# A two-layer graph network on one core: longer lags in the edge stage, norms moved ahead in the tile periods, and a block of VectorE work spread over eight steps

## The chip, the cores and the metric

The kernel runs on one core of one Trainium2 chip. A time is the device time of one execution in microseconds (us). Five engines of the core matter here: TensorE (PE in the profile, with its weight loads as PEld), VectorE (DVE), ScalarE (ACT), GpSimd (POOL) and SyncE (SP, which only issues transfers). Each works through its own instructions in the order in which they stand in the program, and waits on semaphores for the others. PSUM is where TensorE writes its results; a PSUM tile can be written again only when VectorE or ScalarE has read it.

## The reference, cut to what matters

625 nodes with 1024 features (`x`), 10,000 edges (`src`, `dst`), everything in float32. Layer 0 adds a graph attention (edge scores over 4 heads), a linear attention (16 heads of 64) and then a ternary feed-forward block to `x`. Layer 1 adds a two-step neighbour mean (SAGE), a linear attention and a mixture of experts.

```
# layer 0, graph attention
msg = xl[src] + xr[dst]
e   = einsum('ehd,hd->eh', where(msg > 0, msg, 0.2 * msg), att)
p   = exp(e - m[dst]);  alpha = p / (segment_sum(p, dst)[dst] + 1e-16)
out = segment_sum(alpha[..., None] * xl[src], dst).reshape(n, 256) @ W_up
# linear attention, both layers: qf, kf = elu(.) + 1
z   = 1.0 / (einsum('bthd,bhd->bth', q, k.sum(axis=1)) + eps)
out = einsum('bthd,bhdm->bthm', q, kv) * z[..., None] @ W_o + b_o
# the layers
xn = layernorm(x);  x = x + gnn0(xn, edges) + mix0(xn)
x  = x + ffn0(layernorm(x))                  # quantised activations, ternary weights
xn = layernorm(x);  x = x + sage(xn, edges) + mix1(xn)
x  = x + moe(layernorm(x))
```

## The kernel before, in words

`attempt` (the function under the launch) computes all of it; the nodes are cut into five tiles of 125 rows. Until the second half of layer 1 the order of the instructions on every engine is written out by hand. The helper `do` (class `Stream`, line 173) carries it: each call first runs the next waiting step of the calls before it (`after`, `after2`: reading out a PSUM tile, as a rule), then issues its own TensorE work (`pe`). So VectorE's and ScalarE's work on a result stands one or two steps behind the matmuls that made it.

**Edge stage** (lines 550 to 670; about 50 to 410 us of the span). TensorE makes keys and values of the linear attention (`key`, `value`), counts edges with one-hot matmuls (`pct`), makes the attention states (`states`), and then goes through eight queries and answers (`query`, `answer`). Beside that the 10,000 edges are scored in 40 groups of two columns of 128 edges (the last is 16 edges). Each group needs four indirect gathers on GpSimd (`ga`, `gb`, line 573), five VectorE instructions (`score_group`, line 577, and `score`, 553), one exponential on ScalarE (line 560) and two indirect scatters into `table` in DRAM on GpSimd (`scatter`, 584). The function `work` (607) places them: every step of TensorE credits an estimate of its time, and with every 8.0 us of credit one beat is issued.

```
while beat["us"] >= 8.0 * beat["g"] and beat["g"] < len(groups) + 3:
    ...
    if 2 <= g < len(groups) + 2:
        score_group(g - 2)
    for j in range(G):
        if g < len(groups): gather(g, j)
        if g >= 3: scatter(g - 3, j)
```

So a group is gathered in beat g, scored in beat g+2 and scattered in beat g+3. The buffers `ga` and `gb` exist four times: the gathers of a group wait until the group four before it is scored. Scatters follow each other in `table`: each waits until the one before it has landed. `self_loops` (596) writes the diagonal of `table` in beats 1 to 5. `states` reads each of its four PSUM tiles with three VectorE instructions (lines 288 to 291). `answer` takes a reciprocal of 128x626 on VectorE.

**Tile periods** (lines 937 to 988; about 430 to 630 us). After the last scatter GpSimd loads `table` back tile by tile (`load_table`), VectorE multiplies it with the edge counts (`weigh`, five instructions on 125x500), TensorE sums with it (`sums`), turns the result (`turn_sums`) and multiplies it with `W_up` into the same PSUM tile that holds the linear attention's output product (`mixed`, then `up_again`). In period p the kernel runs the sums of tile p, the feed-forward block of tile p-1 (`ffn`: `p1` norm and quantisation on VectorE, `f1` transposes, `f2` to `f4` matmuls with their read-outs) and the second norm of tile p-2 (`p5` on VectorE, `f5` transposes into `xnT1`). `spacer` puts two pieces of other TensorE work into each period: halves of `mixed` of tile p+2, or from p = 3 on a `key` and a `value` of layer 1. Two PSUM tiles (`ps1`) of one bank and three (`ps2`) of two banks serve all of this.

**Layer 1's answers** (lines 1038 to 1055; about 735 to 850 us). Eight queries and answers again. Beside the first two answers VectorE and ScalarE make the ten blocks `xnh`, `xnl` (normalised rows as a high and a low part, `split`, line 1016), five blocks beside each; then TensorE sums over neighbours (`pa`). `degrees` (993) makes the reciprocals of the node degrees earlier.

From 850 us on (second half of layer 1, attention and experts) nothing is touched by the change.

Of the kernel before, what the change touches and what calls it, by code (L numbers as in the profile page):

```python
# [52 lines left out]
def attempt(ctx: ExitStack, tc: tile.TileContext, w: dict, out: bass.AP, shifted: bool):  # L53
# [161 lines left out]
    class LinearAttention:  # L215
# [59 lines left out]
        def states(self):  # L275


            kf, v, kv = self.kf, self.v, self.kv[-1]

            def state(a):  # L280
                def pe():
                    hold["pkv", a] = ps1("pkv")
                    group(hold["pkv", a][:, :129], [(kf[:, t, a * 128:(a + 1) * 128], v[:, t, a, :])
                                                    for t in range(NT)])

                def after():
                    pkv = hold.pop(("pkv", a))
                    nc.vector.tensor_tensor(kv[:, a, 0:128], pkv[:, 0:128], blockmask, op=ALU.mult)
                    ks = mix.tile([128, 1], FP, tag="ks", name="ks", bufs=2)
                    nc.vector.tensor_copy(ks, pkv[:, 128:129])  # L290
                    nc.vector.tensor_scalar(kv[:, a, 128:256], blockmask, ks, None, op0=ALU.mult)

                do(None, pe, after)
                self.work(3.0)

            return [lambda a=a: state(a) for a in range(4)]
# [38 lines left out]
    with ExitStack() as st0:  # L335
        main = st0.enter_context(tc.tile_pool(name="l0", bufs=1))
        goT = main.tile([128, 2, N], FP, name="goT")
# [7 lines left out]
        with ExitStack() as edges:  # L345
# [207 lines left out]
            def score(dst, m, n, p):  # L553
# [4 lines left out]
                if not shifted:  # L558
                    nc.vector.tensor_scalar(dst, dst, LIMIT, None, op0=ALU.min)
                    nc.scalar.activation(dst, dst, AF.Exp)  # L560
# [35 lines left out]
            def self_loops(t):  # L596
# [3 lines left out]
                score(own[:, t:t + 1, :], m, 1, P)  # L600
                nc.vector.tensor_copy(xl1[:, t, :, 0:64], xlr[:, t, 0:256].rearrange("p (h e) -> p h e", h=4))
# [5 lines left out]
            def work(us):  # L607
                beat["us"] += us
                while beat["us"] >= 8.0 * beat["g"] and beat["g"] < len(groups) + 3:
# [4 lines left out]
                    if 2 <= g < len(groups) + 2:  # L614
                        score_group(g - 2)
                    for j in range(G):
                        if g < len(groups):
                            gather(g, j)
                        if g >= 3:
                            scatter(g - 3, j)  # L620
# [28 lines left out]
            for f in states[1]:  # L649
                f()  # L650
            for m in range(KC):
                if m + 1 < KC:
                    lin.query(m + 1)
                lin.answer(m, oT)
# [11 lines left out]
            while beat["g"] < len(groups) + 3:  # L666
# [36 lines left out]


        def mixed(t):
            for c in range(2):
                def pe(c=c):
                    if c == 0:
                        hold["px", t] = ps2("px1")
                    for k in range(KC):  # L710
                        nc.tensor.matmul(hold["px", t][:P, c, :], lhsT=oT[:, k, nodes(t)], rhs=wo[c](k),  # L711
                                         start=(k == 0), stop=False)

                yield lambda pe=pe: do(None, pe)
# [57 lines left out]
        def turn_sums(t):  # L772
# [6 lines left out]
            def after():  # L779
                nc.scalar.activation(goT[:, :, nodes(t)], hold["pt"][:, 0:2, :P], AF.Copy)  # L780
# [3 lines left out]
        def up_again(t):  # L784
            px = hold.pop(("px", t))

            def pe():
                for c in range(2):
                    for k in range(2):
                        nc.tensor.matmul(px[:P, c, :], lhsT=goT[:, k, nodes(t)],  # L790
# [34 lines left out]
        def ffn(t):  # L825
# [5 lines left out]
            hT = room[:, 256:384].bitcast(BF).rearrange("p (k n) -> p k n", k=2)  # L831

# [64 lines left out]
            def p5():  # L897
                stats(t, mv1, rs1)
                nc.vector.tensor_scalar(xq, x[:, t, :], mv1[:, t, 0:1], rs1[:, t:t + 1],
                                        op0=ALU.subtract, op1=ALU.mult)  # L900

            def f5():
                do(None, lambda: transpose_in(xnT1, t, xq))
# [6 lines left out]
        for f in mixed(0):  # L910
            f()
# [25 lines left out]
        for p in range(NT + 2):  # L937
# [3 lines left out]
            if p >= 2:  # L941
                made_of[p - 2][5]()
            spacer(p, 0)
            if p >= 2:
                made_of[p - 2][6]()
            if 1 <= p <= NT:
                made_of[p - 1] = ffn(p - 1)
                made_of[p - 1][0]()
            if p + 1 < NT:
                weigh(p + 1)  # L950
            if p == 0:
# [3 lines left out]
                                       lambda us: None, nc.gpsimd)  # L955
            if p + 2 < NT:
# [5 lines left out]
            if p < NT:  # L962
                sums(p)
            if 1 <= p <= NT:
                made_of[p - 1][1]()
                do()
                made_of[p - 1][2]()
# [25 lines left out]
    def degrees():  # L993
# [8 lines left out]
        def after():  # L1002
            nc.vector.tensor_scalar(halves(dinv), hold["pdeg"][:, :, :HN], 1.0, None, op0=ALU.max)
            if not shifted:
# [3 lines left out]
            nc.vector.reciprocal(dinv, dinv)  # L1008
            own = mix.tile([P, NP], FP, tag="qe", name="own", bufs=1)[:, 0:N].rearrange("p (t n) -> p t n", t=NT)
            nc.vector.tensor_tensor(own, dinv[:P, 0:N].rearrange("p (t n) -> p t n", t=NT),  # L1010
                                    ident[:P, :P].unsqueeze(1).to_broadcast([P, NT, P]), op=ALU.mult)
            nc.vector.tensor_reduce(dinvT, own, AX.X, ALU.add)

        do(None, pe, after)

# [22 lines left out]
    xnh = []  # L1038
    for m in range(KC):
        if m + 1 < KC:  # L1040
            lin1.query(m + 1)
        lin1.answer(m, oT)
        if m < 2:

            parts = [midp.tile([P, NT, 512], NUM, tag="mid", name="xnh")]
            parts.append(sage.tile([P, NT, 512], NUM, name="xnl") if m else
                         midp.tile([P, NT, 512], NUM, tag="mid", name="xnl"))
            for t in range(NT):
                xh = mix.tile([P, 512], FP, tag=("kb", "ke")[t % 2], name="xh", bufs=1)
# [780 lines left out]
```

## Time and profile before

| | |
|---|---|
| time, median of 3 runs | 2252.4 us (2249.21 to 2257.08) |
| the profiled execution's own time | 2253.43 us |
| its span, first to last instruction | 2251.6 us |
| TensorE matmuls busy | 2128.0 us (95%) |
| VectorE busy | 757.5 us (34%) |
| ScalarE busy | 195.6 us (9%) |
| GpSimd busy | 347.7 us (15%) |
| mean granted TensorE clock | 0.975 |

The busy times are sums over one execution; the page's second part cuts the span into 40 slices of 56 us and gives each engine's busy share in tenths. A row of waits names the engine and tile that stood still, the work that ended the wait, the total in us, the number of times and the longest. In the order of time ("the timeline") a row has start, duration, engine, line, operation and tiles, and in brackets the idle time of the engine just before it with what ended it. A float32 matmul stands as two rows.

### The profile page before, as it was taken

What the parts mean: (1) busy time and instruction counts of PE and PEld (TensorE: products, weight loads), DVE (VectorE), ACT (ScalarE), POOL (GpSimd) and SP (SyncE); (2) the same over time, 40 slices, a digit from 0 to 9 for tenths busy, and PEclk for the clock granted to TensorE, in tenths of its full rate; (3) what the DMA queues carried; (4) which work ended last, traced back from release to release, by engine and by line L of the source; (5) the groups of instructions that cost most, each with busy time, mean ns of one, the idle gap of its engine ahead of it and who ended that gap; (6) DMA issues with size and microseconds to landing.
All of it is one profiled execution on the core that took longest, in us unless ns stands there. A gap on an engine that the chain in (4) does not pass through costs nothing. (4 is left out here: it accounts for less than half of the span.)

```text
span 2251.6 us, 17442 instructions
## 1 busy us (share of the span) xinstructions
PE 2128.0 (95%) x6934; PEld 1217.9 (54%) x6934; DVE 757.5 (34%) x1305; ACT 195.6 (9%) x334; POOL 347.7 (15%) x351
## 2 busy tenths in 40 slices
PE   8989888888799899999999999999999999999998
PEld 6555455444454568764445776556754444444443
DVE  5878668764522561001013233322111111111112
ACT  2000001012210210000000111110000000000000
POOL 1667767400000040010000000110000000000010
PEclk9989988989999899999999999999999999999999
DMA  9343252521122110231213111030288997898742
GB/s 297 104 144 100 64 189 85 135 69 38 38 85 66 46 57 1 75 116 61 75 38 103 38 38 38 19 102 10 84 315 322 331 331 282 323 331 301 263 148 94
DMA packets 145849, 301.63 MB, mean 134 GB/s; under 512 B 12370, under 2 KB 22436, under 8 KB 145754
## 3 DMA queue, kind: packets, MB, share of 16 engines
q1 hardware_dynamic: 123412, 243.18, 30.2%
q0 software_dynamic: 17664, 47.47, 7.1%
q10 hardware_dynamic: 4678, 9.72, 1.4%
q8 instruction: 58, 0.95, 0.2%
q14 instruction: 37, 0.30, 0.0%
HBM read 277.49 MB, written 22.84 MB: 133 GB/s over the span
## 5 line engine op out<-in xcount | busy, mean ns | idle before, releaser
L129 PE MATMUL pu<-w,xgT 128*128 128x512 f32 x768 | 333.9, 593 | 1.9 <-DVE xgT L1124 1.9
L129 PEld LDWEIGHTS pu<-w,xgT 128*128 128x128 f32 x768 | 144.1, 190 | 174.7 <-issue 171.9
L129 PE MATMUL pyb<-w,hb 128*128 128x512 f32 x384 | 174.3, 599 | 2.4 <-ACT yb L104 2.1
L129 PE MATMUL pq<-xnT,w 128*128 128x313 f32 x512 | 150.7, 457 | 16.4 <-ACT qf L311 11.4
L129 PE MATMUL pk<-w,xnT 128*125 128x512 f32 x320 | 142.6, 599 | 4.7 <-DVE x L893 4.7
L129 PE MATMUL pv<-w,xnT 128*125 128x512 f32 x320 | 140.7, 592 | 0.0
L129 PEld LDWEIGHTS pq<-xnT,w 128*128 128x128 f32 x512 | 104.6, 205 | 61.6 <-ACT qf L311 13.3
L129 PE MATMUL p<-tT,w 128*128 128x313 f32 x512 | 136.3, 428 | 0.4 <-DVE tT L1124 0.4
L1664 DVE TENSOR_TENSOR su<-pu,su 128x512 f32<-128x512 f32 x24 | 16.6, 691 | 314.6 <-ACT su L1663 314.6
L129 PEld LDWEIGHTS pyb<-w,hb 128*128 128x128 f32 x384 | 69.9, 189 | 90.9 <-issue 74.8
L129 PEld LDWEIGHTS p<-tT,w 128*128 128x128 f32 x512 | 96.8, 190 | 37.8 <-issue 1.2
L129 PEld LDWEIGHTS pk<-w,xnT 128*125 128x125 f32 x320 | 60.1, 190 | 79.6 <-issue 72.9
L129 PEld LDWEIGHTS pv<-w,xnT 128*125 128x125 f32 x320 | 59.4, 188 | 71.1 <-issue 70.5
L587 POOL DMA_INDIRECT table<-es,at x79 | 84.0, 1063 | 57.8 <-issue 24.2
L1647 POOL DMA_INDIRECT xg<-rows_d,slots x12 | 11.3, 943 | 524.8 <-PE pxg L1654 449.0
L573 POOL DMA_INDIRECT ga<-xl_d,si x79 | 80.7, 1021 | 31.7 <-issue 20.7
L573 POOL DMA_INDIRECT gb<-xr_d,di x79 | 80.6, 1021 | 24.1 <-issue 23.5
L711 PE MATMUL px<-w,oT 128*125 128x512 f32 x160 | 73.3, 614 | 5.5 <-DVE oT L330 3.8
L1020 DVE TENSOR_TENSOR z<-pz,z 125x512 fp32r<-125x512 f32 x10 | 6.9, 692 | 196.8 <-ACT z L1018 196.8
L129 PE MATMUL px<-w,hT 128*125 128x512 f32 x160 | 70.3, 592 | 0.0
L129 PE MATMUL px<-w,oT 128*125 128x512 f32 x160 | 70.3, 592 | 0.0
L129 PE MATMUL ph<-meanT,w 128*128 128x313 f32 x256 | 70.1, 426 | 0.0
(357 smaller groups left out, 2582.1 us busy)
## 6 DMA issues: line engine op xcount, KB each, us to landing
w<-in_eW_dram SPq DMA_DIRECT2D x144, 1024.0 KB
w<-in_L_Wk_dram SPq DMA_DIRECT2D x8, 1024.0 KB
w<-in_L_Wv_dram SPq DMA_DIRECT2D x8, 1024.0 KB
w<-in_L_Wq_dram SPq DMA_DIRECT2D x8, 1024.0 KB
w<-in_L_Wo_dram SPq DMA_DIRECT2D x8, 1024.0 KB
w<-in_W_self_dram SPq DMA_DIRECT2D x8, 1024.0 KB
w<-in_W_neigh_dram SPq DMA_DIRECT2D x8, 1024.0 KB
w<-in_sW_dram SPq DMA_DIRECT2D x8, 1024.0 KB
```

What stands on the lines that cost most here:

```text
L129: nc.tensor.matmul(dst, lhsT=lhsT, rhs=rhs, start=(i == 0), stop=(i == len(pairs) - 1))
L573: nc.gpsimd.indirect_dma_start(out=dst[0:p, j, :], out_offset=None, in_=src[:, :], in_offset=bass.IndirectOffsetOnAxis(ap=ix[0:p, lo + j:l ...
L587: nc.gpsimd.indirect_dma_start(out=table[:, :], out_offset=bass.IndirectOffsetOnAxis(ap=at[0:p, lo + j:lo + j + 1], axis=0), in_=es[0:p, l ...
L711: nc.tensor.matmul(hold["px", t][:P, c, :], lhsT=oT[:, k, nodes(t)], rhs=wo[c](k), start=(k == 0), stop=False)
L1020: nc.vector.tensor_tensor(low, src, high.bitcast(FP), op=ALU.subtract)
L1647: nc.gpsimd.indirect_dma_start(out=xg, out_offset=None, in_=rows_d[:, :], in_offset=bass.IndirectOffsetOnAxis(ap=slots[:, b:b + 1], axis=0))
L1664: nc.vector.tensor_tensor(su, pu[:, 0, :], su, op=ALU.mult)
```

## The change

Five edits to the schedule; no arithmetic is added or dropped.

1. Edge stage: a beat comes every 7.6 us of credit; a group is scored three beats after its gathers, its exponential is a step of its own one beat later, and its scatters come five beats after the gathers.
2. `states`: ScalarE copies each PSUM tile into `raw`; VectorE does the masking for all four at once, one step later.
3. Six of the eight parts of tile 0's `mixed` are issued before the last answer of layer 0.
4. Tile periods: `p5` and then `p1` stand at the head of a period, `weigh` and the additions of the bias `bo` come after `f2`; `p5` writes into buffers of its own (`xn1`) and `f5`'s two read-outs are both on ScalarE. `goT` becomes a tile of its own for each node tile.
5. Layer 1: the ten blocks of `xnh`, `xnl` are spread over six answers (2, 2, 2, 2, 1, 1); the degrees' reciprocals (`inverses`) move behind the block of answer 5; the last answer stands after the first of the neighbour sums.

```diff
 # states
                 def after():
-                    pkv = hold.pop(("pkv", a))
-                    nc.vector.tensor_tensor(kv[:, a, 0:128], pkv[:, 0:128], blockmask, op=ALU.mult)
-                    ks = mix.tile([128, 1], FP, tag="ks", name="ks", bufs=2)
-                    nc.vector.tensor_copy(ks, pkv[:, 128:129])
-                    nc.vector.tensor_scalar(kv[:, a, 128:256], blockmask, ks, None, op0=ALU.mult)
-                do(None, pe, after)
+                    nc.scalar.activation(raw[:, a, :], hold.pop(("pkv", a))[:, 0:129], AF.Copy)
+                def after2():
+                    mask = blockmask.unsqueeze(1).to_broadcast([128, 4, 128])
+                    nc.vector.tensor_tensor(kv[:, :, 0:128], raw[:, :, 0:128], mask, op=ALU.mult)
+                    nc.vector.tensor_tensor(kv[:, :, 128:256], raw[:, :, 128:129].to_broadcast([128, 4, 128]), mask,
+                                            op=ALU.mult)
+                do(None, pe, after, after2 if a == 3 else None)
 # work
-                while beat["us"] >= 8.0 * beat["g"] and beat["g"] < len(groups) + 3:
+                while beat["us"] >= 7.6 * beat["g"] and beat["g"] < len(groups) + 5:
...
-                    if 2 <= g < len(groups) + 2:
-                        score_group(g - 2)
+                    if 4 <= g < len(groups) + 4:
+                        lo, n, p = groups[g - 4]
+                        exp(es[0:p, lo:lo + n, :])
+                    if 3 <= g < len(groups) + 3:
+                        score_group(g - 3)
...
-                        if g >= 3:
-                            scatter(g - 3, j)
+                        if g >= 5:
+                            scatter(g - 5, j)
 # layer 0's answers
             for m in range(KC):
                 if m + 1 < KC:
                     lin.query(m + 1)
+                else:
+                    for f in mixed(0, range(6)):
+                        f()
                 lin.answer(m, oT)
 # ffn
             def p5():
                 stats(t, mv1, rs1)
-                nc.vector.tensor_scalar(xq, x[:, t, :], mv1[:, t, 0:1], rs1[:, t:t + 1],
-                                        op0=ALU.subtract, op1=ALU.mult)
+                for h in range(2):
+                    nc.vector.tensor_scalar(xn1[h], x[:, t, h * 512:(h + 1) * 512], mv1[:, t, 0:1], rs1[:, t:t + 1],
+                                            op0=ALU.subtract, op1=ALU.mult)
             def f5():
-                do(None, lambda: transpose_in(xnT1, t, xq))
+                def pe():
+                    for h in range(2):
+                        p = ps1("ptr").rearrange("p (c n) -> p c n", c=4)
+                        for c in range(4):
+                            nc.tensor.transpose(p[:, c, :P], xn1[h][:, c * 128:(c + 1) * 128], ident[:P, :P])
+                        nc.scalar.activation(xnT1[:, 4 * h:4 * h + 4, nodes(t)], p[:, :, :P], AF.Copy)
+                do(None, pe)
 # the tile periods
                 made_of[p - 2][5]()
+            if 1 <= p <= NT:
+                made_of[p - 1] = ffn(p - 1)
+                made_of[p - 1][0]()
             spacer(p, 0)
             if p >= 2:
                 made_of[p - 2][6]()
-            if 1 <= p <= NT:
-                made_of[p - 1] = ffn(p - 1)
-                made_of[p - 1][0]()
-            if p + 1 < NT:
-                weigh(p + 1)
...
+            if p < NT:
+                sums(p)
+            if 1 <= p <= NT:
+                made_of[p - 1][1]()
+                do()
+                made_of[p - 1][2]()
+            do()
+            if p + 1 < NT:
+                weigh(p + 1)
             if p + 2 < NT:
                 load_table(p + 2)
             for t in range(2 * p, min(2 * p + 2, NT)):
                 for c in range(2):
                     xc = x[:, t, c * 512:(c + 1) * 512]
                     nc.vector.tensor_tensor(xc, xc, bo[c][:P], op=ALU.add)
-            if p < NT:
-                sums(p)
-            if 1 <= p <= NT:
-                made_of[p - 1][1]()
-                do()
-                made_of[p - 1][2]()
 # layer 1's answers
+    def rows_of(c, t):
+        xh = mix.tile([P, 512], FP, tag=("kb", "ke")[t % 2], name="xh", bufs=1)
+        nc.vector.tensor_scalar(xh, x[:, t, c * 512:(c + 1) * 512], mv1[:, t, 0:1],
+                                rs1[:, t:t + 1], op0=ALU.subtract, op1=ALU.mult)
+        split(xh, xnh[c][0][:, t, :], xnh[c][1][:, t, :])
+
+    for m in range(KC - 1):
+        lin1.query(m + 1)
+        lin1.answer(m, oT)
+        for _ in range(2 if m < 4 else 1):
+            if rows_left:
+                rows_of(*rows_left.pop(0))
+        if m == 5:
+            inverses()
...
     for k in range(KC):
+        if k == 1:
+            lin1.answer(KC - 1, oT)
```

In the changed order of instructions GpSimd has eleven scatters in a row behind the last gathers (seven before) and four fewer among them; SyncE's transfers keep their order. VectorE's order in a period with a layer 1 `key` becomes `p5`, `p1`, then the `key`'s bias addition `kb`.

## The prediction

> **What bounds the kernel now.** I read the page first, then the stages, then who TensorE waits for, then the order of time around those waits.
>
> ```profile
> PE 2128.0 (95%) x6934; PEld 1217.9 (54%) x6934; DVE 757.5 (34%) x1305; ACT 195.6 (9%) x334; POOL 347.7 (15%) x351
> PEclk9989988989999899999999999999999999999999
> ```
>
> TensorE is the bound overall; all dips of its clock lie in the first 850 us. The windows by stage put a size on that (columns: PE, PEld, DVE, ACT, POOL busy, granted clock, DMA share, GB/s):
>
> ```profile
> 148.00:265.00 117.00, 98.75 (x342) 57.19 (x341) 88.65 (x186) 9.22 (x24) 85.77 (x83) 0.93 0.33 101
> 264.00:408.00 144.00, 119.53 (x392) 79.00 (x392) 104.92 (x128) 14.53 (x32) 97.02 (x95) 0.88 0.35 116
> 430.00:640.00 210.00, 172.87 (x620) 94.28 (x619) 105.02 (x208) 37.86 (x51) 4.62 (x9) 0.92 0.18 53
> 640.00:850.00 210.00, 194.73 (x656) 120.86 (x655) 93.77 (x113) 25.49 (x38) 27.46 (x17) 0.94 0.20 68
> 850.00:2251.00 1401.00, 1384.64 (x4244) 765.45 (x4242) 237.70 (x375) 86.26 (x138) 46.35 (x51) 1.00 0.43 154
> ```
>
> Added gap by gap from the timeline, TensorE idles 43.0 us in the edge stage, 37.1 in the tile periods and 15.3 around layer 1's answers. After most gaps of 2.2 us and more its clock runs at half for slices of 3.4 us; by the trace's clock record matmuls were busy for 42.0, 20.3 and 18.5 us in such slices, and half of that is lost: 21.0, 10.2 and 9.2 us. So 64, 47 and 24.5 us are there to be had, 136 in all. The waits say who ends the gaps:
>
> ```profile
> PE ptr L845 <- DVE go L767: 14.7, 4, 6.1
> PE pkv L129 <- DVE ks L290: 13.3, 4, 8.3
> PE pq L129 <- ACT qf L311: 11.4, 3, 5.0
> PE ptr L845 <- DVE room L823: 11.3, 4, 6.4
> PE po L129 <- DVE oT L330: 6.7, 3, 3.7
> ```
>
> All are read-outs late on a queue, but VectorE (34%) is not full: something else stands in its queue. In the edge stage it is a gather that has not landed (timeline, then the tile view of the gathers: total and times):
>
> ```profile
> 159.82 0.69 DVE L581 TENSOR_TENSOR ga<-ga,gb 128x512 f32<-128x512 f32 x1 [6.26 <-issue]
> 163.92 2.49 PE L129 MATMUL pkv<-v,kf 125*128 125x129 f32 x10 [8.35 <-DVE ks L290]
> ...
> DVE ga L581: 41.4, 12
> ```
>
> Behind that stands GpSimd. Its transfers' rows start 1.27 (gather after gather), 1.25 and 1.30 us apart (medians), and in the timeline group 8 starts at 119.42, group 36 at 361.66: 8.65 us a group. The waits over 0.3 us in this stretch add to 17.3 us; without them it is 8.03. GpSimd's queue is full 93% of the time. **The edge stage is bound by GpSimd's issue of transfers**, not by VectorE's order alone. Its tail:
>
> ```profile
> 392.99 0.97 POOL L587 DMA_INDIRECT table<-es,at  x1 [1.40 <-DMA table<-es,at]
> 395.86 0.96 POOL L587 DMA_INDIRECT table<-es,at  x1 [1.90 <-DMA table<-es,at]
> 409.24 0.89 POOL L163 DMA_DIRECT2D tb<-table  x1 [1.76 <-PE pm L129]
> ```
>
> Without gathers between them each scatter waits for the last one to land: seven in 18.97 us (390.27 to 409.24), 2.71 each. Only then is `table` loaded back.
>
> In the tile periods VectorE's own order is the obstacle (period 3):
>
> ```profile
> 524.33 0.69 DVE L247 TENSOR_TENSOR kb<-pk,bk_t 125x512 f32<-125x512 f32 x1 [3.76 <-PE pk L129]
> 532.24 4.83 DVE L730 TENSOR_TENSOR pT<-tb,CT 125x500 f32<-125x500 f32 x5
> 538.57 1.07 PE L845 MATMUL ptr<-ident,room 125*128 125x125 f32 x4 [5.03 <-DVE go L767]
> ```
>
> `weigh` (4.83 us) stands before `go`, which frees the PSUM tile that the second transpose needs.
>
> **The edge stage, worked out.** Lags and the `raw` copies let VectorE and ScalarE wait less; the number of transfers stays. So I follow GpSimd. Start: gathers at 55.6 as before. Until group 8 the ring of four buffers sets the pace: gathers of g need the scoring of g-4, now one beat back instead of two. VectorE passed old beats 6 and 7 at 97 and 111; new beat 7 (53.2 us of credit, 6.65 old beats) comes near 106, the scoring takes 3.6, so group 8 starts near 110 (9 earlier, mostly because no early scatter waits for `table<-own` or `es`). Then 31 groups of 8.03: 359. Of the 17.3 us of waits, those ended by `es`, `qf` or shown as "issue" should go (the exponential is one beat older, the scatter two); about 8 to 10 are scatters waiting for a scatter's landing while weights stream in, and stay: group 39 starts at 368 (before: 387.7), the tail at 370.5. The tail is now eleven scatters: 29.8 us. The first `tb` load issues near 400.5, only 9 us earlier. It lands after 9.0 us (median of its tile view), its second piece is issued 0.9 later: 411; `weigh(0)` 4.9: the sums start near 415.5. TensorE itself: the score of group 38, 3.65 us, runs before answer 7's reciprocal (0.84+4.07+0.81), so oT is complete near 378; weight sums end near 387 (score of group 39, 2.2, three reductions 6.7); then `mixed` of tiles 1 and half of 2, 20.8, and a half-clock slice 1.7: 409. So the load chain decides: 415.5 against 429.78. **Gain 14** (4 to 31, the two ends by the rivals A and B). `mixed` of tile 0 ahead of the last answer fills 10.3 us of TensorE under the reciprocal; it shortens the path only if GpSimd doesn't bound it, and counts nothing here. The states' twelve small instructions (0.28+0.15+0.29 each four) become two of 0.7 on VectorE and four copies on ScalarE: hidden as long as ScalarE isn't behind a late `es`.
>
> [...] In this stage GpSimd's transfers last 0.96 (median) and up to 1.45 us, the longer ones beside one-hot and scoring instructions of VectorE. [...] at the trace's worst, 1.45 instead of the mean 1.03, they would add 95. The change packs VectorE's work only 5% denser, so I keep the mean of the trace.
>
> **The tile periods.** Now `go` no longer waits for `weigh`, and `p1` follows `p5` without waiting for the transposes. Durations of the period-2 and 3 rows: statistics 1.28+0.21, root with hand-over 0.36, norm halves 0.54 each, norm 0.81, reduction 1.22, quantisation 0.75. Period 1: second transpose at 459.5 instead of 461.7, the end 3.3 earlier. Period 2: `xq` ready at 488.4, sums end at 491.1, `go` 0.8, second transpose at 492.1 instead of 498.8; no half-clock slice behind it; `weigh` ends at 503, `hT` at 504.7, still under `up_again`: 8.5. Period 3: here the `key` is the spacer, and its `kb` (frees the PSUM tile for the second transpose of `f5`) stands behind `p1`: 526.9 instead of 525.0, a new stall of 2.0; ScalarE then makes `ke` and `kb` (0.63 each) before the two `xnT1` copies that VectorE shared: 1.5 more before the sums. Second transpose at 534.4 instead of 538.6; `weigh` delays `v` and the next transpose by 1.0: 3.2 less a half-clock slice: 2.2. Period 4 had no `weigh`: -0.9. Period 5: 3.6. Period 6: -1.3. **Gain 15** (8 to 21). The fewer table loads of ScalarE (1.28 each) and the longer life of `xn1` and `goT` are hidden. `load_table` keeps its place behind `weigh` on GpSimd's queue; its buffers are then long free (before, 22.7 us of waiting cost nothing).
>
> *A rule on the stalls.* The trace halves the clock after a gap of 2.23 us (530), 2.43 (395) and 2.90 (459), not after 1.3 or 1.4. [...] by the trace each costs 1.7. I take the trace.
>
> **Layer 1's answers.** Five blocks in a row (1.95 us each, VectorE waiting for ScalarE in each) delayed z and oT: gaps 13.8, states 1.5, clock 9.2. Spread, an answer has on VectorE two blocks 3.9, qf 0.81, z to oT 5.8, against 10.55 us of TensorE: starting 1.65 us after the query's end that is some 0.4 late, four times: 1.6. Answer 5 gets `inverses` as well (reciprocal 4.07, product and reduction 1.6): oT is 4.1 late once, with a slice 1.7. The last answer no longer waits for its reciprocal: the first neighbour sum (5.3) covers it. GpSimd's additions of `b1` and `L1_bo` now start some 16 us later, under the neighbour sums; nobody reads `x` before 1000. Left: 7.5 of 24.5. **Gain 16** (10 to 21).
>
> **Sum.** 14 + 15 + 16 = 45 off the profiled execution's 2253.4 (span 2251.6): 2208.4. The median of the runs is 1.0 lower: **2207**.
>
> **The rivals.** (A) GpSimd keeps 8.65 us a group, waits and all: group 39 at 378, the first `tb` load at 410.5, the sums at 425.5; edge gain 4: 2217. For: part of the waits is the transfers' own; against: the longest ones were for `es` or `table<-own`. (B) GpSimd runs at its medians, 7.65: the load at 383.5, the sums at 398.5, edge gain 31: 2190. (C) In the periods the late `kb` and ScalarE's copies eat the gain: 0 there, 2222. (D) The ring: with one beat instead of two between a buffer's release and its next gather, GpSimd waits for VectorE in every group. Between groups 4 and 8 it ran at 9.2 us a group already. Each us more a group moves the table load, which has no cover left, by 31 us: from 9.5 on the whole gain of 45 is gone, at 10.0 it is 61 us over the forecast: 2268, slower. Against: once GpSimd is late, the buffer that it needs next was scored three groups ago. (E) No effect: every us taken from a wait comes back at the table load: 2252.
>
> **Chances.** Forecast 0.56 (2193 to 2216), A 0.14, B 0.14, C 0.10, D 0.04, E 0.02. One tenth is left out on either side: 2186 to 2230. 0.3% (7 us) is what this measurement can tell from no change. Faster by more 0.94, within 0.02, slower 0.04.
>
> **What would show it.** Group 39's gathers near 368 and the first `tb` load near 400 (A: 412, B: 385); TensorE idle before the first sums, with the clock at half behind it; no wait `ptr <- go` over 1 us, new ones `ptr <- kb` near 2 us in periods 3 to 5; one wait of about 4 us at `po` in answer 6. Wrong if GpSimd waits for `ga` buffers in most groups, or if the stages after 850 us change.

## The result, and the profile after

2240.8 us (2239.2 to 2245.4, five runs) against 2257.0 (2249.2 to 2257.6) for the kernel before: 0.9938 of its time, interval 0.9924 to 0.9952. The gain is 16 us, not 45, and the time lies above the forecast range of 2186 to 2230. The profiled executions lie closer together: their span went from 2251.6 to 2240.2, 11.4 us less. From the page after (engines' busy time; TensorE's clock in 40 slices) and the windows by stage:

```profile
PE 2124.3 (95%) x6934; PEld 1214.5 (54%) x6934; DVE 754.2 (34%) x1265; ACT 193.5 (9%) x349; POOL 346.7 (15%) x351
PEclk9998999898899999999999999999999999999999
```

```profile
148.00:265.00 117.00, 96.41 (x358) 56.33 (x356) 85.62 (x172) 9.46 (x27) 85.86 (x84) 0.93 0.32 100
264.00:422.00 158.00, 129.07 (x423) 81.69 (x424) 114.89 (x128) 15.64 (x36) 101.72 (x97) 0.89 0.32 104
430.00:640.00 210.00, 186.01 (x635) 103.54 (x634) 113.33 (x223) 33.79 (x52) 9.69 (x18) 0.92 0.26 75
640.00:850.00 210.00, 196.51 (x722) 125.44 (x721) 95.68 (x95) 26.24 (x44) 26.92 (x16) 0.98 0.17 60
850.00:2240.00 1390.00, 1373.30 (x4166) 753.86 (x4164) 234.19 (x367) 86.26 (x138) 46.42 (x51) 1.00 0.43 156
```

Only layer 1's window has a clearly better clock (0.94 to 0.98); the edge stage and the tile periods keep theirs. Cut at the same events in each trace (us; "first pk" is the first key product, "sums" are the products `pg`, a tile period ends with its `pdn`, and `ph` is the first product behind layer 1's answers):

| kernel | first pk to first sums | sums to end of period 1 | end of period 1 to last pdn | to layer 1's first query | that query to first ph | rest |
|---|---|---|---|---|---|---|
| before | 384.6 | 48.1 | 141.3 | 109.2 | 137.0 | 1386.3 |
| after | 383.1 | 51.2 | 130.7 | 109.6 | 131.9 | 1386.2 |

The gains are 1.5, -3.1, 10.6, -0.3, 5.1 and nothing behind; the first pk itself came 2.4 us later, with the first loads (it lies between 45.0 and 48.6 in all runs). The sum is the span's difference, 11.4.

**Edge stage.** GpSimd's queue at the end of the stage, then VectorE's and TensorE's first work with the table (timeline):

```profile
389.05 1.02 POOL L592 DMA_INDIRECT table<-es,at  x1 [0.30 <-issue]
...
410.47 1.81 POOL L592 DMA_INDIRECT table<-es,at  x1 [1.89 <-DMA table<-es,at]
...
410.94 1.23 DVE L725 TENSOR_SCALAR gu<-raw 128x2048 bf16<-128x2048 f32 x1
...
413.69 2.31 POOL L592 DMA_INDIRECT table<-es,at  x1 [1.41 <-DMA table<-es,at]
...
414.66 1.23 DVE L725 TENSOR_SCALAR gu<-raw 128x2048 bf16<-128x2048 f32 x1
...
417.91 1.78 POOL L592 DMA_INDIRECT table<-es,at  x1 [1.91 <-DMA table<-es,at]
...
418.38 1.23 DVE L725 TENSOR_SCALAR dn<-raw 128x2048 bf16<-128x2048 f32 x1
...
421.40 0.89 POOL L163 DMA_DIRECT2D tb<-table  x1 [1.70 <-DMA table<-es,at]
...
429.57 4.85 DVE L743 TENSOR_TENSOR pT<-tb,CT 125x500 f32<-125x500 f32 x5 [9.97 <-DMA tb<-table]
...
430.68 0.43 PE L129 MATMUL pg<-xl,pT 125*125 125x65 f32 x2
...
431.62 0.43 PE L129 MATMUL pg<-xl,pT 125*125 125x65 f32 x2 [0.51 <-DVE pT L743]
```

The gathers of group 39, the last, start at 386.7 (before 387.7, forecast 368), the table load at 421.4 (before 409.2, forecast 400). From the first of the eleven scatters in a row to the load it takes 32.4 us (forecast 29.8). The sums then start before `pT` is complete and pause four times for 0.5 us, once for each further block; TensorE's clock is at half from 435.9 to 442.7.

**Tile periods**, period 3 (timeline):

```profile
520.58 0.68 DVE L247 TENSOR_TENSOR kb<-pk,bk_t 125x512 f32<-125x512 f32 x1
...
521.32 0.65 PE L924 MATMUL ptr<-ident,xn 125*128 125x125 f32 x4 [1.93 <-DVE kb L247]
...
523.12 5.21 PE L129 MATMUL pg<-xl,pT 125*125 125x65 f32 x30 [1.16 <-ACT xnT L925]
```

`go` is no longer late (longest wait of `ptr` for it 0.6). The stall at `kb` has the forecast size, 1.93 or 1.94, in periods 3, 4 and 5. But the slow slices behind it, by the trace's clock record, last 10.2 and 13.7 us in periods 3 and 4 (524.6 to 534.9, 558.8 to 572.4); in period 5 it is 3.4.

**Layer 1's answers** (the ten blocks now stand beside six answers). First two steps of the loop; then a block and the reciprocals of answer 5, with what TensorE's answer 6 waits for (timeline):

```profile
754.65 0.81 DVE L333 TENSOR_TENSOR oT<-po,z 128x626 f32<-128x626 f32 x1
...
755.57 0.78 ACT L312 ACTIVATE qe<-pq,bq 128x626 f32<-128x626 f32 x1 [6.58 <-DVE oT L333]
...
766.49 0.81 DVE L333 TENSOR_TENSOR oT<-po,z 128x626 f32<-128x626 f32 x1
...
767.42 0.78 ACT L312 ACTIVATE qe<-pq,bq 128x626 f32<-128x626 f32 x1 [6.58 <-DVE oT L333]
...
805.70 2.35 POOL L1089 TENSOR_TENSOR x<-x,b_t 125x1024 f32<-125x1024 f32 x1 [9.23 <-DVE xh L1072]
...
806.32 2.28 DVE L1047 TENSOR_TENSOR xnl<-xh,xnh 125x512 fp32r<-125x512 f32 x1 [0.70 <-ACT xnh L1045]
...
812.61 2.63 DVE L1039 TENSOR_TENSOR own<-dinv,ident 125x625 f32<-125x625 f32 x1
...
817.05 1.40 PE L129 MATMUL pd<-qf,kv 128*128 128x313 f32 x4 [3.99 <-DVE z L331]
...
822.07 2.46 PE L129 MATMUL po<-qf,kv 128*128 128x313 f32 x4 [3.62 <-DVE oT L333]
```

ScalarE's `qe` of a later query waits for VectorE's `oT`: `qe` and `z` are one buffer (`mix`, tag "qe", one copy). So a query's `qe` can't be written before the answer two steps back is complete. The step is 11.85 us (767.42 less 755.57), longer than TensorE's 10.55.

### The profile page after: what moved, and what is told of

Same layout as the page of the kernel before. It is cut to its first block, busy times and chain, and to the rows that moved or that the text cites. A ratio compares the mean times of both kernels' runs of the same rounds, so it can differ in the third digit from the quotient of the medians.

```text
span 2240.2 us, 17398 instructions
## 1 busy us (share of the span) xinstructions
PE 2124.3 (95%) x6934; PEld 1214.5 (54%) x6934; DVE 754.2 (34%) x1265; ACT 193.5 (9%) x349; POOL 346.7 (15%) x351
## 5 line engine op out<-in xcount | busy, mean ns | idle before, releaser
L129 PE MATMUL pq<-xnT,w 128*128 128x313 f32 x512 | 143.2, 440 | 11.0 <-DVE v L268 9.7
L129 PEld LDWEIGHTS pq<-xnT,w 128*128 128x128 f32 x512 | 99.8, 196 | 54.1 <-DVE v L268 10.5
L1680 POOL DMA_INDIRECT xg<-rows_d,slots x12 | 11.4, 947 | 524.7 <-PE pxg L1687 449.0
```

The lines of the kernel that those rows point to most:

```text
L129: nc.tensor.matmul(dst, lhsT=lhsT, rhs=rhs, start=(i == 0), stop=(i == len(pairs) - 1))
L1680: nc.gpsimd.indirect_dma_start(out=xg, out_offset=None, in_=rows_d[:, :], in_offset=bass.IndirectOffsetOnAxis(ap=slots[:, b:b + 1], axis=0))
```

## The experiments

Theory: the scatters of the edge stage wait for each other, so the lags bring nothing there; the clock makes the stall at `kb` dear; layer 1's answers run in a loop over a shared buffer. The runs were made in four batches. In two of them (edge_old, no_gb, f5_ps2, l1_loop; tiles_l1, tail9, old_lags_mixed_late, l1_z), called disturbed below, the edge stage was some 40 to 50 us longer, in the kernel before too (2310 and 2305 us as a whole, against 2255 and 2257 in the other two). It isn't a chip's property: one chip ran an undisturbed batch (ctrl's) and a disturbed one (tiles_l1's). The disturbed runs are read by the stages behind the edge stage, and whole times only within their batch. The stages come from one profile of each kernel.

**The edge stage.** edge_old: old lags.

```diff
-  while beat["us"] >= 7.6 * beat["g"] and beat["g"] < len(groups) + 5:
+  while beat["us"] >= 8.0 * beat["g"] and beat["g"] < len(groups) + 3:
...
-      exp(es[0:p, lo:lo + n, :])          # group g - 4
...
-      score_group(g - 3)
+      score_group(g - 2)
+      exp(es[0:p, lo:lo + n, :])          # group g - 2
...
-      scatter(g - 5, j)
+      scatter(g - 3, j)
```

> The changed kernel, with the lags of the edge stage as before: a beat every 8.0 us, scored two beats after the gathers, exponential behind the scoring, scattered three beats after; all other edits stay. Theory 1 (GpSimd's queue sets the end of the stage, 8.7 us a group whatever the lags, and each scatter behind the last gather adds 2.7 to 2.9): four scatters fewer stand in the tail, so the first load of the table issues near 410 instead of 421.4, and the first sums (pg) come 5 to 12 us earlier than 430.7; whole time 2229 to 2236. Rival (the longer lags do help, by keeping VectorE and ScalarE from waiting): the pace of the groups falls back to 9 us and more, the first sums come near or behind 431, and the whole time is the changed kernel's 2240.8 or up to 10 above it.

Measured 2285.3 (0.9907 of before, 0.9884 to 0.9931); first pk to sums 428.3 us, with 434.0 and 434.3 in the two kernels of that batch that kept the new lags. The disturbance is larger than the effect. In an undisturbed batch the same lags (`best`, below) gave 390.3 against 383.9 for the changed kernel (ctrl): 6.4 later, where theory 1 said 5 to 12 earlier. Counted to the end of period 1, before any other edit of `best` acts, it is 435.1 in both, so the lags by themselves bring nothing. no_gb: no second gather; the kernel leaves the rows `xr[dst]` out.

```diff
-  for dst, src, ix in ((ab[g][0], xl_d, si), (ab[g][1], xr_d, di)):
+  for dst, src, ix in ((ab[g][0], xl_d, si),):
```

> The changed kernel without the second gather of each column: the rows xr[dst] are not fetched, and the score takes the row of xl twice (this part of the computation is changed). GpSimd issues 79 transfers fewer of 305. Theory 1 (GpSimd's issue bounds the edge stage): at 1.3 us each some 105 us less for GpSimd, so that TensorE and VectorE set the pace instead: the groups come at the beats of the program, the last gather near 330 instead of 386.7, the first sums 25 to 60 us earlier. Rival (VectorE's order, or the landing of the scatters one behind another, bounds it): gathers weigh little, the first sums move by less than 10 us.

Measured: 346.6 us from first pk to sums, 82 to 88 less than the others of its batch (disturbed), and still 37 less than the undisturbed 383.1 of the kernel after, inside the 25 to 60 of theory 1; last gather at 336.4; whole time 2199.0 (0.953, 0.9497 to 0.9564). GpSimd then waits 58 us between groups 8 and 39 and no longer sets the pace. With all gathers in it, GpSimd's queue does bound the stage.

two_tables: every second column goes to another table.

```diff
+  table2 = dram.tile([128 * 3080, 4], FP, name="table2")
...
-  out=table[:, :],
+  out=(table, table2)[j][:, :],
```

> The changed kernel, with every second column scattered into a second table in DRAM that nobody reads (the weights of those edges are left out of the result). A scatter then waits for the landing of the scatter two before it. Theory 1 (in the tail each scatter waits for the one before it to land, 2.8 us, and the first load of the table waits for all): the eleven scatters of the tail take 15 to 18 us instead of 31, the waits for a scatter's landing fall from 32 us to under 10, the pace of the groups comes to 8.1 to 8.5 us, and the first load of the table issues 15 to 30 us earlier relative to the first gathers. Rival (GpSimd itself needs 2.8 us for a scatter that no gather precedes): the tail stays at 30.

GpSimd's end in this kernel (timeline):

```profile
370.03 0.96 POOL L593 DMA_INDIRECT table<-es,at  x1 [0.61 <-issue]
371.30 1.15 POOL L593 DMA_INDIRECT table<-es,at  x1 [0.30 <-issue]
373.85 0.96 POOL L593 DMA_INDIRECT table<-es,at  x1 [1.40 <-DMA table<-es,at]
...
384.93 0.90 POOL L163 DMA_DIRECT2D tb<-table  x1 [1.71 <-DMA table<-es,at]
```

Its waits, first in the kernel after, then here (us in total, times, longest):

```profile
POOL table L592 <- DMA table<-es,at: 32.6, 18, 4.2
```

```profile
POOL table L593 <- DMA table<-es,at: 1.7, 2, 1.4
```

Group 8 to group 39 takes 251.3 us, 8.11 a group, against 8.78 after and 8.65 before; the eleven scatters, from the first to the load, 17.8 instead of 32.4 us (15 to 18 forecast); first pk to sums 363.4. The load comes 37 us earlier than after, more than the 15 to 30 of the forecast. Its whole time (2262.6, ratio 1.0034) isn't compared: the other data give the experts more work (832 products `pu` instead of 768), and the rest behind the first ph is 45 us longer. Between groups 8 and 39 what GpSimd's waits exceed 0.3 us by adds to 19.1 before, 20.3 after, and to nothing here (counting waits over 0.45), and before and after most lie at nearly the same places, 135 to 175, 291 to 303, 324 and 382 us. The trace's landing times say why: nine of the ten waits before, and ten of the twelve after, come behind a scatter that took 3.6 to 7.3 us to land, where the median is 2.2. In two_tables scatters land as late (up to 6.2 us), but nobody waits for them. With the scatters' chain cut the waits are gone: they were a scatter's waits for the landing of the scatter ahead. This is the cause.

**The tile periods.** f5_ps2 and f5_pair put both transposes of `f5` into one two-bank tile from period 3 on; f5_ps2 leaves each copy behind its own four transposes, f5_pair (shown, cut) issues all eight first.

```diff
+  both = ps2("ptr5") if t else None
+  halves_of = []
   for h in range(2):
-      p = ps1("ptr").rearrange("p (c n) -> p c n", c=4)
+      p = both[:, h, :] if t else ps1("ptr")
+      p = p.rearrange("p (c n) -> p c n", c=4)
...
-      nc.scalar.activation(xnT1[:, 4 * h:4 * h + 4, nodes(t)], p[:, :, :P], AF.Copy)
+      halves_of.append(p)
...
+  if t:
+      for h in range(2):
+          nc.scalar.activation(xnT1[:, 4 * h:4 * h + 4, nodes(t)], halves_of[h][:, :, :P], AF.Copy)
```

> The changed kernel, with both transposes of f5 in one two-bank PSUM tile (ps2) from period 3 on, so that the second need not wait for the release of the key's tile by kb. Theory 1 (the stalls at ptr <- kb, 1.93 + 1.16 us, and the half-clock slices behind them cost periods 3 to 5 some 3.4 and more each): these waits go, periods 3 to 5 are 8 to 12 us shorter together, the sum of the half-clock slices between 520 and 605 falls from 27 us to under 10; whole time 2229 to 2233. Rival (another read-out is late in the same place, the copies of xnT1 on ScalarE or go): the stall turns up at pg or at the next ptr, and the gain is under 4 us.

> The changed kernel, with both transposes of f5 in one two-bank PSUM tile from period 3 on, all eight transposes ahead of the two copies. Theory 1 (the second transpose waits for kb, and the pair of gaps of 1.93 and 1.16 us brings a half-clock slice of 10 us): no gap over 1.5 us between 520 and 605 us, no slice with over 4 us of matmuls in it, and each of periods 3 to 5 is 6 to 8 us shorter: 15 to 24 us less from the first sums to the last pdn. Rival (the clock drops anyway, or the copies on ScalarE and the sums' own wait take the place of the gap): under 6 us less.

Who TensorE waited for in the periods, f5_ps2:

```profile
PE ptr L926 <- ACT xnT L927: 11.2, 3, 3.7
```

The half-written tile ties the second transpose to ScalarE's copy of the first, which stands behind `ke` and `kb`: one gap of 3.7 us instead of 1.93 and 1.16, and the same loss (130.8 us from period 1 to the last pdn; whole time 2289.7, 0.9925 of before, 0.9899 to 0.9951). So its rival came true. f5_pair took the wait away. The window 520 to 540 in ctrl (the changed kernel in that batch) and in f5_pair, busy PE, PEld, DVE, ACT, POOL, then the clock:

```profile
520.00:540.00 20.00, 16.71 (x71) 12.67 (x71) 8.09 (x22) 2.69 (x5) 0.00 (x0) 0.74 0.00 1
```

```profile
520.00:540.00 20.00, 18.95 (x93) 11.90 (x92) 14.47 (x28) 5.36 (x8) 0.00 (x0) 1.00 0.01 1
```

More work fits into the same 20 us at full clock. Periods 3 and 4 last 29.5 us instead of 37.4; period 5 gains only 1.0, with a new wait of 1.99 us at `pgu` in it (none over 1.5 was forecast). The end of period 1 to the last pdn takes 113.8 instead of 130.5; from the first sums on it is 14.7 less, just short of the 15 to 24 of the forecast, because period 1, where the sums pause, took 2.0 more. Whole time 2224.7 (0.9861, 0.9846 to 0.9877) against 2244.0 of ctrl (0.9952, 0.9940 to 0.9965).

> The changed kernel, unchanged, so that the other kernels are compared with it on one chip. All theories: the stages from the first sums on last as in its first profile (tile periods 182 us less the half-clock slice at their start, first query of layer 1 to the first ph 132 us); the edge stage shows how far its 383 us are this chip's.

ctrl repeats the stages of the kernel after within 0.8 us.

**Layer 1's answers.** l1_loop: `z` in a buffer of its own and `inverses` back at the end of the read-out in `degrees`; l1_z: the buffer alone.

```diff
-  z = mix.tile([128, NP], FP, tag="qe", name="z", bufs=1)
+  z = (self.room or mix).tile([128, NP], FP, tag="z" if self.room else "qe", name="z", bufs=1)
...
+  inverses()                # in degrees
...
+  lin1.room = sage
...
-  if m == 5:
-      inverses()
```

> The changed kernel, with z in a buffer of its own in layer 1 (it shared one with qe), and with the degrees' reciprocals back in front of layer 1's answers. Theory 1 (a loop qe, qf, two blocks, z, reciprocal, oT, qe of 11.9 us an answer, closed by the shared buffer, is longer than TensorE's 10.55 us): queries and answers run at TensorE's pace, the waits po <- oT of 1.3 us in answers 0 to 3 and the 7 us at answer 6 go, and the stretch from the first query to the first ph takes 121 to 125 us instead of 131.9; whole time 2230 to 2234. Rival (VectorE's work in the answer is itself too long, buffer or not): the waits keep over 1 us in answers 0 to 3, and only the wait at answer 6 shrinks: 4 to 6 us.

> The changed kernel, with only z of layer 1 in a buffer of its own; the degrees' reciprocals stay at answer 5. Theory 1 (two separate causes: the loop over the shared buffer costs 1.3 us in each of answers 0 to 3 and at answer 6, and the reciprocals cost some 6 of the 7.6 us at answers 5 and 6 and the slow clock behind): the stretch from layer 1's first query to the first ph is 124 to 128 us, between 131.9 and the 121 of both edits. Rival (the loop is all, the reciprocals fit once the loop is broken): 121 to 122. Second rival (the reciprocals are all): 130 to 132.

What ScalarE's `qe` waited for between the first query and the first ph, after, then l1_loop:

```profile
ACT qe L312 <- DVE oT L333: 50.3, 6, 15.8
ACT qe L312 <- PE pq L129: 21.4, 2, 13.3
```

```profile
ACT qe L313 <- PE pq L129: 57.8, 8, 13.3
```

All eight now wait for their own product. The stretch is 119.3 us in l1_loop (131.9 after) and 123.2 in l1_z, just under its 124 to 128: the buffer is worth 8.7, the reciprocals some 4 more (with both edits the stretch lies between 117.8 and 121.1 in the eight kernels below). How much of the 4 is GpSimd's additions, beside which a subtraction and `own` took 2.28 and 2.63 us in the kernel after instead of 0.69 and 0.81, isn't separated. l1_loop: 2276.8 against 2310.5 of before (0.9890, 0.9859 to 0.9922).

**Together.** `best`: old lags with f5_pair and l1_loop. tiles_l1 (and tiles_l1_b in an undisturbed batch): the new lags with these two. old_lags_mixed_late and lags_mixed_late: all of tile 0's `mixed` behind the last answer again. edge_before: also the old `states`. tail9 (tail9_b): scatters four beats behind, and the weight sums' three reductions one each behind answers 4 to 6.

> The changed kernel with four edits: the lags and the beat of the edge stage as before, f5 in one two-bank PSUM tile with its transposes ahead of its copies, z of layer 1 in a buffer of its own, the degrees' reciprocals back in front of the answers. If all three causes hold (scatters in the tail, the wait for kb with its slow clock, the loop over the shared buffer), the sum is 5 + 18 + 12 = 35 us under the changed kernel of the same chip. If only the loop holds, 12; if the longer lags do help, 5 to 10 less than that sum.

> The changed kernel with its own lags, and with the three edits behind the edge stage alone: f5 in one two-bank PSUM tile with its transposes ahead of its copies, z of layer 1 in a buffer of its own, the degrees' reciprocals in front of the answers. Theory 1 (the three causes add up and the lags are worth what the first sums showed, 431.3 against 438.6 us with the old lags): 22 us less from the first sums to the last pdn, 11 less from layer 1's first query to the first ph, so 2205 to 2213, 2 to 9 under the kernel with the old lags. Rival (what is taken from the tile periods comes back in the edge stage or at their start, as a half-clock slice): 2214 to 2222.

> The same kernel as tiles_l1, with the scatters four beats behind the gathers instead of five, and the three reductions of the weight sums one each behind answers 4 to 6 of layer 0, where VectorE waits for gathers. Theory 1 (after the last gather two things end the edge stage together: the row of scatters before the table load, and VectorE's weight sums before TensorE's last 48 products): two scatters fewer are 5.6 us, the weight sums 4 us; the first table load issues near 416, pm 4 us earlier, and the first sums come 3 to 6 us earlier than in tiles_l1. Rival (the pace of the groups suffers from scatters that wait for an exponential, or VectorE's reductions delay scores and so gathers): the last gather comes 3 or more later, and nothing is gained.

> The kernel of `best` (old lags), with all of tile 0's mixed behind the last answer of layer 0, as it stood before the change. Theory 1 (mixed ahead of the last answer delays that answer by 12 us on TensorE; on VectorE the scores of the last groups and the weight sums then stand behind its reciprocal): pm comes 6 to 8 us earlier, near 408, and the first sums 4 to 7 us earlier than 438.6; 2208 to 2211. Rival (VectorE waits there for the last gathers anyway, so the order does not matter): pm moves by under 2 us, whole time 2213 to 2216.

> The kernel of tiles_l1 again, as the base of this batch: all edits of the change, with f5 in one two-bank PSUM tile, z in its own buffer and the degrees' reciprocals in front. If the edge stage is as in the first profiles (383 to 385 us from the first pk to the first sums): 2208 to 2216. If it is longer by some 50 us in all kernels of this batch, before too, the differences below stand only where they are over 10 us.

> As tiles_l1_b, with the whole edge stage as before the change: old lags, beat and states, all of mixed behind the last answer. Theory 1 (the edits of the edge stage together are worth next to nothing, since GpSimd's scatters wait for each other in both): within 3 us of tiles_l1_b. Rival a (the lags are worth 6 to 7 us, as the first sums of the kernel with old lags showed): 5 to 8 us slower. Rival b (they cost, by the longer row of scatters): 3 to 6 us faster.

> As tiles_l1_b, with all of tile 0's mixed behind the last answer of layer 0. Theory 1 (with the new lags the row of scatters and the table load end the stage, not TensorE): within 2 us. Rival a (mixed ahead of the answer fills TensorE's wait for the reciprocal): 4 to 8 us slower. Rival b (it delays the last answer and with it VectorE's weight sums, as where the lags are the old ones): 3 to 6 us faster.

> As tiles_l1_b, with the scatters four beats behind the gathers instead of five, and the three reductions of the weight sums one each behind answers 4 to 6 of layer 0. Theory 1 (the row of scatters before the table load, and VectorE's weight sums before TensorE's last products, end the stage together): first table load 5 to 6 us earlier, first sums 3 to 6 us earlier, 2204 to 2212. Rival (scatters then wait for exponentials, and the pace falls): last gather 3 us or more later, nothing gained.

| kernel | median us | ratio to before | first pk to sums | sums to end of period 1 |
|---|---|---|---|---|
| best | 2214.6 | 0.9812 (0.9797 to 0.9827) | 390.3 | 44.8 |
| tiles_l1_b | 2212.8 | 0.9802 (0.9783 to 0.9821) | 384.2 | 52.9 |
| edge_before | 2207.9 | 0.9788 (0.9773 to 0.9803) | 386.3 | 44.8 |
| lags_mixed_late | 2211.3 | 0.9807 (0.9791 to 0.9823) | 382.4 | 53.2 |
| tail9_b | 2208.2 | 0.9786 (0.9772 to 0.9800) | 380.2 | 52.6 |
| tiles_l1 | 2248.7 | 0.9746 (0.9712 to 0.9781) | 437.0 | 44.9 |
| tail9 | 2254.9 | 0.9777 (0.9744 to 0.9811) | 441.1 | 44.9 |
| old_lags_mixed_late | 2245.9 | 0.9753 (0.9719 to 0.9787) | 427.9 | 44.8 |

Three of the eight rows, the last, are from the disturbed batch. `best` is 29.4 under ctrl; 35 was the sum if all three causes held. From the end of period 1 on all eight agree within 2 us to the last pdn (113.6 to 115.0) and within 4 in layer 1's answers (117.8 to 121.1). All edits of the edge stage together, tiles_l1_b against edge_before, bring 2.1 us up to the sums and lose 8.1 in the period after. The kernel after, with the same edge stage, shows there the four pauses of 0.5 us at `pT` and the clock at half from 435.9 to 442.7. The medians differ by 4.9 in favour of the old stage, with overlapping intervals: rival b's size, but not certain. `mixed` alone is within 2 us, as theory 1 said. With the old lags it does delay the last answer (`best`, timeline):

```profile
408.92 6.67 DVE L707 TENSOR_REDUCE part<-raw 128x1 f32<-128x2048 f32 x3
...
415.65 0.59 PE L129 MATMUL pm<-part,ones 128*128 128x3 f32 x2 [5.97 <-DVE part L707]
```

In edge_before `pm` comes 4.8 us earlier after the first pk (362.5 against 367.3), but there `states` differs too. old_lags_mixed_late fell into a disturbed batch, so this effect alone wasn't settled. tail9_b shows the row of scatters: the load issues 370.5 us after the first pk instead of 374.3 (3.8 earlier, 5 to 6 forecast), the sums start 4.0 earlier (3 to 6 forecast), with the pace unchanged. In the disturbed batch tail9 was the slower of the two, with a pause of 19.9 us before one query, longer than any in the others of that batch.

edge_before (2207.9) and tail9_b (2208.2) beat both kernels: 49 us under before, 33 under the change.

## Why the prediction was wrong, step by step

Three terms of the sum were too large. The edge stage gained 1.5 us instead of 14 (and started 2.4 late), the tile periods 7.5 instead of 15, layer 1's answers 5.1 instead of 16.

- **Bound by GpSimd: right** (no_gb). **31 groups at 8.03 us and half of the waits: wrong**; group 39 comes 19 us behind its forecast. Group 8 is 4.4 of it (114.4 for 110). The pace without waits was nearly right (8.11 in two_tables, 2.5 us in 31 groups). Most of it, 11 us, is the waits: 20.3 instead of the 9 or so that I kept. I let the half go that the trace put down to `es`, `qf` or "issue". All but one of these (a gather's, 1.2 us) came behind a scatter that landed late, with a later event's name on them, and the lags don't touch that. This is rival A, 8.78 measured for its 8.65, and its load time was still 9 to 11 us early. Rival D didn't show: between groups 8 and 39 no gather waited over 0.3 us.
- **Eleven scatters for 29.8 us: 2.6 short.** The first eight took the forecast 2.7 each. The last three ran beside VectorE's `ternary` instructions (128x2048) and took 1.81, 2.31 and 1.78 us, where the median scatter takes 1.00; each ended 0.1 us behind the end of such an instruction (412.28, 416.00 and 419.69 behind 412.17, 415.89 and 419.61). That is longer than the 1.45 us that I had as the trace's worst. For the gathers, beside scoring and one-hot instructions, keeping the mean of the trace was right: it stayed (1.02 before and after).
- **The load chain decides: right**, but the sums' start was the wrong mark. They start on the first block of `pT` and pay the wait in period 1, with a half-clock slice behind it: forecast 3.3 gained there, 3.1 lost. Where the sums don't have to pause, period 1 takes 44.8 us instead of before's 48.1 (no_gb, two_tables, `best`): there the order of the instructions does bring its 3.3.
- **`go` and the order of the norms: right.** Period by period, 1 to 5, the gain was -3.1, 9.3, 1.5, -4.2 and 4.0 us; 3.3, 8.5, 2.2, -0.9 and 3.6 were forecast. With f5_pair's edit the order is worth 27.5 us from the end of period 1 to the last pdn.
- **The stall at `kb`: right in size** (1.93 and 1.16 for 2.0 and 1.5), **its clock priced too low:** 5.0 and 6.4 us lost in the slices of periods 3 and 4 (half of 10.06 and 12.74 us of matmuls) instead of 1.7 each; in period 5 the 1.7 held (half of 3.12). The trace before already had a shorter pause with a slow slice behind it than the 2.2 us that I took as the least: 1.92 us at 761.2, with the clock at half from 763.3, ahead of the next pause at 765.4.
- **Layer 1, 16 us: wrong**, 5.1 measured. I priced an answer by VectorE's queue (0.4 late) and missed that `qe` waits for `z`'s buffer; the loop makes it 1.3. Behind the reciprocals there are three waits (3.99 and 3.62 in answer 6, 2.26 in answer 7), not one of 4.1: I had put GpSimd's additions under the neighbour sums, but they ran beside the blocks and the reciprocals, and there the subtraction and the `own` product took 2.28 and 2.63 us instead of 0.69 and 0.81. l1_z and l1_loop show the two parts, 8.7 and some 4 us. The clock's gain, 9.2 to 3.3, came as hoped.

## What to carry to other kernels

Before pricing a schedule, list the buffers that its stages share: here the one copy that `qe` and `z` share made a loop of two engines' queues, and its 11.85 us, not TensorE's 10.55, were the pace. When a wait is put down to a short instruction of another engine, see whether the waits stay at the same places under another cause, and look at the landing of the transfer ahead; here that was the older, slower event behind them. Price a stall with the clock that follows it (5.0 us were lost behind the 1.93 and 1.16 of period 3), and mark a stage's end where its last wait is paid, not where its first instruction starts.

## What the runs showed of the hardware

- Half-clock slices came with pauses of under 2 us that stood close together. In the kernel after the clock was at half for 10.2 us from 524.6, behind pauses of 1.93 and 1.16 us (from 519.4 and 522.0); for 13.7 us from 558.8, behind one of 1.94 (from 556.8) and with one of 0.73 inside the slice (from 559.8); and for 6.8 us from 435.9, behind the four of 0.5 in the sums (431.1 to 434.5). f5_ps2's single pause of 3.7 us cost the same as the pair (10.2). In period 5, where no sums follow, the pair brought 3.4 us (after) or 6.8 (ctrl) and the single pause 3.4. So the pauses alone didn't give the length of the slice; what does is open.
- In the kernel after four VectorE instructions with two float32 operands in SBUF that started beside one of GpSimd's additions ran longer and ended 0.55 to 0.67 us behind its end: the subtractions at 794.73 and 806.32 (2.29 and 2.28 us; 0.69 without it; the second ended at 808.60, the addition at 808.05), `own` at 812.61 (2.63; 0.81 in the kernel before; 815.24 and 814.58) and `qf` at 823.62 (1.40; 0.81 without it). `oT` and `z`, which read a PSUM tile, and the reciprocals kept their 0.81 and 4.07 us beside such additions.
- A scatter landed 2.2 us after its start in the median, but up to 7.3 us where weights streamed in (a DMA share of 0.66 at 150 to 175 us in the kernel after, 0.85 at 284 to 304; 0.23 at 200 to 250, where all landed within 2.5).
- In the disturbed batches VectorE stood still for long stretches while TensorE issued one count product every 0.7 to 2.1 us and GpSimd's transfers went on every 1.3 us (f5_ps2, 226 to 249.6 us: 23.6). No wait in the trace explains it; its cause is open.
